# Row recurrence after a group norm: a second row of the first half inside the statistics stage, and a last row of the second half by itself

## The chip, the cores and the metric

The kernel runs on one core of a Trainium2 chip. A core has five engines with instruction queues of their own: TensorE (PE, matrix products; its weight loads are listed as PEld), VectorE (DVE), ScalarE (ACT), GpSimd (POOL) and SyncE (SP, which here only issues DMAs). Each engine works through its own instructions in the order in which they were written, and waits where an operand is not there yet. The metric is the time of one execution in device microseconds.

## The reference, cut to what matters

```python
x = x + conv_ref(gn(x), W_is, b_is, W_ss, b_ss)      # x: 8 x 96 x 128 x 128, float32

def gn(v):                     # group norm over (3 channels, all rows, all pixels) of one image, 32 groups
    return (v - mean) / sqrt(var + 1e-5)

def conv_ref(X, ...):
    its = masked 1x3 convolution of every row of X (96 -> 384 channels)
    h = c = 0
    for each of the 128 rows:  # a scan from top to bottom
        gates = conv1x3(h, W_ss) + its[row]           # 96 -> 384 channels along the row
        f, i, o = sigmoid(...); g = tanh(...)         # 96 channels each
        c = f * c + i * g
        h = o * tanh(c)
        out[row] = h
```

Two things set the shape of the work. The statistics of an image need all its pixels before the first row can be normalised. And the rows are a chain: the products of row r+1 need the h of row r, in all pixels and channels.

## The kernel before, in words

**Halves and half steps.** The eight images are two halves (s = 0: images 0 to 3, s = 1: images 4 to 7), which are independent chains. A row of one half is a half step; its index n counts both halves alternately, `n = 2 * row + s`, so n runs from 0 to 255. While one half waits for its activations, TensorE works on the other. One half step has a gate tile of 128 x 512 in each of three PSUM banks, A, B and C (forget, input and output gates, with a third of g in each). The pixels of a row are kept as even and odd halves of 256 columns (4 images x 64).

**A half step** (class `HalfStep`) consists of: the products of the normalised input P, Q, E (`p_`, `q_`, `t_`, tile xs); the products of h, "1" and "2" (with the sum vs and the difference vf of even and odd h, made by `total` S and `difference` F) and "0" and "3" (with the shifted differences vd, `shifted` D, on POOL); a copy cp of the bank's first half, and lo/hi, a sum and a difference that turn the bank into even and odd pixels (`copy`, `even`, `odd`); then ta and si (tanh, sigmoid on ACT), fg, gt, ce, th, ou (f times c, i times g, the new c, its tanh, h) and re (x plus h). All products are written in line 475, in float32; each matmul call shows as two instructions in the profile.

**The order of the work** is written out by hand and as strings. `PERIOD` is the order for one half step of the main loop, `LAST` that for the last: a name such as `3C'` is part 3 of bank C of the half step before, `''` two before, `+` the one after, `<` and `>` take the lower or upper 64 rows of TensorE, a and b are even and odd pixels. `W1`, `W2`, `W3`, `U` and `X` stand where the normalised rows of the next block of four rows are prepared (function `prepare`, lists `FIRST`, `LATER`, `SHARED`): on POOL (`widen`, `add_pixels`, `subtract_pixels`) and partly on ACT (line 308).

**The statistics stage.** Before the main loop every image is read once from HBM: six chunks of 1 MB for each (24 slots of 512 columns), in a ring of six buffers (line 938). A chunk's slots go through `bn_stats` on DVE (line 950), or a whole chunk through ACT (`sums_of`, lines 228 to 230, shares set by `by_act`: chunks 1 and 3 of each image). Of chunks 0, 2 and 4 TensorE picks the first rows (`pick_rows`, line 198). `aggregate` (line 854) ends an image. When the first four images are known, `Scale` makes their scale and shift (lines 264 to 302), and the first half step, n = 0, is run among the statistics of images 4 to 6; the products of n = 2 follow (`next_products`), so that n = 1 and n = 2 can start when the last image is known. Where these things stand is written in the table `events`: `at(i, m)` is the place after slot m of image i. `spin` and `keep_warm` (line 183) are products whose result nobody reads. After the loop `final.deviations()` is TensorE's first step for the last image.

**The main loop** is `do(n, PERIOD)` for n from 2 to 254, then `do(255, LAST)` and six calls behind it for the end of n = 255. In `LAST`, the end of n = 254 and all of n = 255 are interleaved.

Of the kernel before, what the change touches and what calls it, by code (L numbers as in the profile page):

```python
# [21 lines left out]
def kernel(  # L22
# [29 lines left out]
    nc = tc.nc  # L52
    B, C, H, W = x.shape
# [386 lines left out]
    class HalfStep:  # L440


        def __init__(self, n):
            self.n, (self.row, self.s) = n, divmod(n, NH)
# [113 lines left out]
        def sigmoid(self, a, lo=0, hi=BH, t=None):  # L558
            if self.row == 0 and a == 0:
                return  # L560
            gate = self.part(self.ps[a][0:C], lo, hi, t)
            if t == 0 and self.n > NH:
# [4 lines left out]
            nc.scalar.activation(to, gate, AF.Sigmoid)  # L567

        def forget(self):
            f = self.ps[0][0:C]  # L570
            if self.row > 0:
                nc.vector.tensor_mul(f, f, self.c)

        def gated(self, lo=0, hi=BH, t=None):
            to = self.g if self.row > 0 else self.c
# [53 lines left out]
            )  # L629
            hold(diff, self.last)  # L630

        def residual(self):
            s, row = self.s, self.row
            xo = xt[s, row // R][0:C, :, row % R, :].rearrange("p b (j t) -> p t b j", t=2)
            if self.n < NH or self.n == last - 1:
                nc.gpsimd.tensor_add(xo, xo, self.h)
            else:
                residuals.append(nc.vector.tensor_add(xo, xo, self.h))  # L638
# [28 lines left out]
    def beside(s, k, *images):  # L667
# [15 lines left out]
    def work(n):  # L683
        if n < len(FIRST):
            return FIRST[n]
        row, s = divmod(n, NH)
# [33 lines left out]

    def finish(n):
        prepare(n)
        row, s = divmod(n, NH)
# [24 lines left out]
    SPLIT = ("taC", "siB", "gt", "ce", "th", "ou")  # L748
    PARTS = {
# [12 lines left out]
    def do(n, names, by_lanes=False):  # L762

        for name in names.split():
            if name in "UX":
                if n >= NH:
                    prepare(n - NH, name)
# [19 lines left out]

            if part in ("S", "F", "D"):
                at += NH
            if not 0 <= at <= last:  # L790
                continue
            step = half_step(at)
            if name in step.done or whole_name in step.done:
# [9 lines left out]
            if by_lanes and part == "re":  # L803
                finish(at)


# [36 lines left out]
        step.shifted()  # L843
        step.done |= {"S", "F", "D"}

    def begin():
        operands(0)
        do(0, "PA PB QA QB PC QC 1A 2A 1B 2B 1C 2C")

    def at(image, n):  # L850
        return image * NS + n
# [29 lines left out]
        late[0].means()  # L881

    def keep_warm(count):
        unread = late[0].banks[0] if early_done else half_step(1).ps[1]
        spin(1, bst[:, done - 1, :], unread)
        spin(count, wt[0][:, 0:256], unread)
# [1 line left out]

    early_done = []
    events = {  # L890
        at(4, 5): lambda: (late.insert(0, Scale(0, 0, BH)), begin_scale()),
        at(4, 6): squares,
        at(4, 8): lambda: (
            late[0].scale(), late[0].shift(), [own_image(0, 0, j) for j in range(BH)]
        ),
        at(4, 13): lambda: shared_rows(nc.scalar, 0, 0, R),
        at(5, 4): begin,
        at(5, 6): lambda: do(0, "cpA cpB cpC"),
        at(5, 17): lambda: do(
            0, "loA hiA EA 0A 3A loB hiB EB 0B 3B loC hiC EC 0C 3C taA taB siB taC siC"  # L900
        ),
        at(6, 4): lambda: (do(0, "gt th ou"), operands(2), do(0, "re")),
        at(6, 6): next_products,
        at(6, 17): lambda: keep_warm(8),
        at(6, 22): lambda: do(2, "cpA cpB cpC"),
        at(7, 5): begin_scale,
        at(7, 7): squares,
        at(7, 8): lambda: (next_row(), spin(8, wt[0][:, 0:256], half_step(1).ps[1])),
        at(7, 12): next_operands,
        at(7, 16): lambda: spin(3, wt[0][:, 0:256], half_step(1).ps[1]),  # L910
        at(7, 20): lambda: (own_row(xw[1], 1, 0, 0, BH - 1), early("1A 2A 1B 2B"), keep_warm(1)),
        at(7, 21): lambda: keep_warm(1),
        at(7, 22): lambda: keep_warm(3),
        at(7, 23): lambda: keep_warm(1),
        at(7, 24): lambda: keep_warm(1),
    }
    for b in range(B - 1):
        events[at(b + 1, 7 if b == 4 else 5 if b == 5 else 4)] = lambda b=b: aggregate(b)
    stats = []
    n = m = 0  # L920
    load_weights()
# [3 lines left out]
    for b in range(B):  # L925
        bst = g_pool.tile([P, NS, 6], F32, tag="bst", name=f"bst{b}")
        records = bst.rearrange("c n s -> c (n s)")
        shares = by_act(b)
        own_stats = NS - sum(shares.values())
        stats.append(records[:, 0 : 6 * own_stats + 3 * len(shares)])  # L930
        xb = x[b].rearrange("c h w -> (c h w)").rearrange("(p q) -> p q", p=P)
        done = 0
        for k in range(QW // CH):
            xc = ring[n % len(ring)]
            pieces = 2 if n == B * QW // CH - 1 else 1
            for piece in range(pieces):
                size = CH // pieces
                nc.sync.dma_start(  # L938
                    xc[:, bass.ts(piece, size)], xb[:, bass.ds(k * CH + piece * size, size)]
                )  # L940
            n += 1
            if k % 2 == 0:
                pick_rows(b, k // 2, xc)
            alone = shares.get(k, 0)
            if alone:
                i = list(shares).index(k)
                sums_of(b, i, xc[:, CH - alone * SN :], records[:, 6 * own_stats + 3 * i :][:, 0:3])
            for j in range(CH // SN):
                if j < CH // SN - alone:
                    nc.vector.bn_stats(bst[:, done, :], xc[:, bass.ts(j, SN)])  # L950
# [68 lines left out]
    step.residual()  # L1019
    finish(last)  # L1020


# [52 lines left out]
```

## Time and profile before

| what | us |
|---|---|
| median of 3 runs (range) | 1966.6 (1965.81 to 1968.24) |
| the profiled execution, its own time | 1967.33 |
| its span in the profile | 1965.5 |
| last chunk of statistics begun by DVE | 128.87 |
| aggregate of the last image ends | 130.87 |
| TensorE's first product for the last image | 132.48 |
| last residual add ends | 1962.13 |

The profile lists busy times by engine, a chain of work that ended last, groups of instructions, and a timeline. A timeline row has the start in us, the duration, the engine, the line, the operation with its output and input tiles, shapes, how many instructions the row merges, and in brackets the idle time of the engine before it and what ended it. In a table by stretches each row has the stretch, its length, the busy time (and instructions) of PE, PEld, DVE, ACT and POOL, the granted clock of TensorE, the busy share of the DMA engines and GB/s.

### The profile page before, as it was taken

How to read it: one execution, taken by the hardware profiler on the slowest of the kernel's cores; microseconds unless marked ns; L12 is line 12 of the kernel's file. 1: busy time of each engine (PE TensorE's matmuls, PEld its weight loads, DVE VectorE, ACT ScalarE, POOL GpSimd, SP SyncE). 2: the span in 40 equal slices, each digit the busy share in tenths (PEclk: the TensorE clock that was granted, in tenths of full speed). 3: DMA queues.
4: the chain of work that ended last, by engine and by line, in shares of the span. 5: the costliest groups of instructions: out<-in, count | busy, mean ns of one | idle time of the engine just before them, and what ended most of it. 6: DMA issues, size and time to landing. Idle time of an engine off the chain costs nothing.

```text
span 1965.5 us, 46244 instructions
## 1 busy us (share of the span) xinstructions
PE 1901.2 (97%) x17492; PEld 1819.2 (93%) x17492; DVE 1794.7 (91%) x4002; ACT 1567.1 (80%) x3494; POOL 1359.4 (69%) x1645
## 2 busy tenths in 40 slices
PE   3699999999999999999999999999999999999998
PEld 0279999999999999999999999999999999999997
DVE  5778999999999999999999999999999999999998
ACT  6777888887888888888888877888887888888777
POOL 3348777777777777777777777777777777777752
PEclk9999999999999999999999999999999999999999
DMA  9993343444334334433433443343344433434411
GB/s 402 421 308 75 88 116 94 105 119 117 82 87 115 97 98 119 119 90 85 107 98 98 119 119 98 82 103 100 95 119 119 101 86 95 109 94 112 119 34 33
DMA packets 101277, 234.64 MB, mean 119 GB/s; under 512 B 5824, under 2 KB 7360, under 8 KB 95040
## 3 DMA queue, kind: packets, MB, share of 16 engines
q1 hardware_dynamic: 101056, 231.70, 43.6%
q8 instruction: 138, 2.26, 0.5%
q14 instruction: 83, 0.68, 0.1%
HBM read 181.34 MB, written 50.33 MB: 118 GB/s over the span
## 4 chain that ended last, share of the span: by engine, by line
PE 93%; DMA 4%; DVE 2%; ACT 1%; issue 0%; SPq 0%; POOL 0%; DVEq 0%; POOLq 0%; ACTq 0%
PE ps L475 92%; DMA xs<-in_x_dram 4%; DVE bst L950 1%; PE ps L183 0%; PE dm L183 0%; ACT g L555 0%; ACT piece L308 0%; DVE ps L551 0%; DVE hx L604 0%; DVE ps L547 0%; SPq L938 0%; DVE vf L621 0%; PE rows L198 0%; ACT th L596 0%; ACT ps L567 0%
## 5 line engine op out<-in xcount | busy, mean ns | idle before, releaser
L475 PE MATMUL ps<-vd,wl 64*128 64x256 f32 (+1 forms) x6092 | 1191.6, 376 | 0.1
L475 PEld LDWEIGHTS ps<-vd,wl 64*128 64x128 f32 (+1 forms) x6092 | 871.9, 186 | 16.7 <-issue 1.3
L475 PE MATMUL ps<-vs,wm 64*128 64x256 f32 (+1 forms) x3054 | 821.3, 376 | 2.4 <-POOL vs L617 2.3
L475 PE MATMUL ps<-vf,wm 64*128 64x256 f32 (+1 forms) x3056 | 766.8, 377 | 1.1 <-DVE vf L621 1.1
L475 PE MATMUL ps<-xs,wx 64*128 64x256 f32 (+1 forms) x3586 | 747.1, 347 | 0.4 <-POOL xs L327 0.4
L475 PEld LDWEIGHTS ps<-xs,wx 64*128 64x128 f32 x3586 | 606.5, 187 | 4.3 <-POOL xs L327 2.3
L567 ACT ACTIVATE ps<-ps 96x256 f32<-96x256 f32 (+1 forms) x767 | 387.8, 506 | 231.5 <-PE ps L475 223.0
L475 PEld LDWEIGHTS ps<-vs,wm 64*128 64x128 f32 (+1 forms) x3054 | 528.8, 186 | 12.9 <-POOL vs L617 2.7
L555 ACT ACTIVATE g<-ps 32x256 f32<-32x256 f32 (+1 forms) x1021 | 468.6, 482 | 25.0 <-PE ps L475 6.0
L475 PEld LDWEIGHTS ps<-vf,wm 64*128 64x128 f32 (+1 forms) x3056 | 459.4, 186 | 20.9 <-DVE vf L621 1.9
L475 PE MATMUL ps<-xs,wt 64*128 64x256 f32 x1528 | 452.8, 377 | 0.4 <-DVE ps L551 0.4
L543 ACT ACTIVATE m<-ps,wl 128x256 f32<-128x256 f32 x766 | 363.0, 474 | 95.0 <-PE ps L475 70.1
L625 POOL TENSOR_TENSOR vd<-hx 128x512 f32<-128x512 f32 x257 | 287.9, 1120 | 180.0 <-DVE vs L617 170.3
L547 DVE TENSOR_TENSOR ps<-m,ps 128x256 f32<-128x256 f32 x768 | 324.3, 423 | 78.8 <-ACT m L543 78.6
L551 DVE TENSOR_TENSOR ps<-m,ps 128x256 f32<-128x256 f32 x768 | 326.9, 426 | 18.7 <-PE ps L475 1.2
L638 DVE TENSOR_TENSOR x<-x,hx 96x512 f32<-96x512 f32 x253 | 341.0, 1348 | 0.0
L310 POOL TENSOR_SCALAR xw<-xr,rstd,nmr 128x512 f32<-128x512 f32 (+1 forms) x255 | 205.6, 806 | 115.0 <-DVE x L638 114.5
L310 POOL TENSOR_SCALAR hx<-x,rstd,nmr 32x512 f32<-32x512 f32 (+1 forms) x249 | 222.4, 893 | 72.9 <-POOL xs L331 52.7
L331 POOL TENSOR_TENSOR xs<-xw 128x512 f32<-128x512 f32 (+1 forms) x254 | 270.9, 1067 | 0.0
L475 PEld LDWEIGHTS ps<-xs,wt 64*128 64x128 f32 x1528 | 266.5, 187 | 2.0 <-DVE ps L551 1.6
L579 POOL TENSOR_TENSOR g<-i,g 96x256 f32<-96x256 f32 x252 | 183.5, 728 | 118.0 <-ACT g L555 110.1
L604 DVE TENSOR_TENSOR hx<-ps,th 96x256 f32<-96x256 f32 (+1 forms) x510 | 190.5, 413 | 1.9 <-ACT th L596 1.8
(101 smaller groups left out, 1505.5 us busy)
## 6 DMA issues: line engine op xcount, KB each, us to landing
xr<-in_x_dram SPq DMA_DIRECT2D x124, 512.0 KB, 6.5
x<-in_x_dram SPq DMA_DIRECT2D x62, 768.0 KB, 5.9
out_dram<-x SPq DMA_DIRECT2D x62, 768.0 KB, 5.2
xs<-in_x_dram SPq DMA_DIRECT2D x31, 1024.0 KB, 12.4
piece<-in_x_dram SPq DMA_DIRECT2D x16, 1024.0 KB, 10.8
x<-in_x_dram SPq DMA_DIRECT2D x62, 256.0 KB, 3.2
out_dram<-x SPq DMA_DIRECT2D x2, 576.0 KB, 3.7
xs<-in_x_dram SPq DMA_DIRECT2D x2, 512.0 KB, 13.3
```

The source lines that it names most:

```text
L310: return engine.tensor_scalar(dst, src, scale, shift, ALU.mult, ALU.add)
L331: nc.gpsimd.tensor_sub(differences, strided(xw[:, 0, :], 0, [(W + 1, n), (J, 2), (1, J)]), strided(xw[:, 0, :], J + 1, [(W + 1, n), (0, 2) ...
L475: made = nc.tensor.matmul(self.ps[a][:, bass.ts(half, HB)][:, cols], weights[rows, bass.ts(a, P)], rhs[rows, cols], start=new, stop=False, ...
L543: nc.scalar.activation(self.m1[a], m1, AF.Identity, bias=column)
L547: nc.vector.tensor_add(self.ps[a][:, 0:HB], self.m1[a], self.ps[a][:, HB:])
L551: nc.vector.tensor_sub(hi, self.m1[a], hi)
L555: nc.scalar.activation(self.part(g, lo, hi, t), self.part(ps, lo, hi, t), AF.Tanh)
L567: nc.scalar.activation(to, gate, AF.Sigmoid)
L579: nc.gpsimd.tensor_mul(to, i, g)
L604: nc.vector.tensor_mul(h, o, th)
L625: diff = nc.gpsimd.tensor_sub(self.operand("vd", 2)[:, :, lo:hi], strided(h, 1, [(BH * JP - 1, 2), (JP, hi - lo), (1, J)]), strided(h, 0, ...
L638: residuals.append(nc.vector.tensor_add(xo, xo, self.h))
```

## The change

1. The first half runs one row ahead of the second (`LEAD = 1`, function `place`): n = -2 and n = 0 are rows 0 and 1 of s = 0 and both stand among the statistics; n = 2 is row 2 of s = 0, beside n = 1, row 0 of s = 1. So n = 254 no longer exists, and the loop ends with n = 253; n = 255, row 127 of s = 1, has no partner.
2. Rows 0 to 3 of the first half are no longer prepared image by image (`own_image`, four rows each) but row by row (`row_of`).
3. The table of events is written anew. `next_products` moves from `at(6, 6)` to `at(7, 6)`. `keep_warm(1)`, four TensorE instructions, stands after every slot from `at(6, 12)` to `at(7, 22)`, but does nothing before `next_products`; the other spins of the loop are gone.
4. ACT takes other chunks: in image 4 and 7 chunks 0 and 3, in image 5 chunk 0 alone, in image 6 chunk 1 and half of chunk 3. The slots left over go to DVE.
5. `LAST` is a new order for the end of n = 253 and all of n = 255, with its steps split by even and odd pixels; its input products (P, Q, E) stand ahead of h, and E is added to both halves of the bank with half weights. The six calls behind the loop are gone.

```diff
     def by_act(b):
-        return {1: CH // SN, 3: CH // SN}
+        shares = (
+            {1: 4, 3: 4},
...
+            {0: 4, 3: 4},
+            {0: 4},
+            {1: 4, 3: 2},
+            {0: 4, 3: 4},
+        )
+        return shares[b]
...
+    LEAD = 1
+
+    def place(n):
+
+        row, s = divmod(n, NH)
+        return row + (LEAD if s == 0 else 0), s
...
         def t_(self, a):
-            if self.n >= last - 1:
-                self.mm(a, 0, wh, self.xs[:, 2].rearrange("p b j -> p (b j)"))
-            else:
+            if 0 < self.n < last:
                 self.own(a, 2)
+                return
+            rhs = self.xs[:, 2].rearrange("p b j -> p (b j)")
+            rows = slice(C2, P) if a == order["B"] else slice(0, C2)
+            for half in range(2):
+                self.mm(a, half, wh, rhs, rows)
...
-        ([], own(1, 1, 3), [(load_rows, 1, 2)]),
+        (shared(0, 2, *SHARED[0]), own(1, 1, 3), [(load_rows, 1, 2)]),
         ([], own(0, 2, 0), []),
     ]
-    LATER = dict(zip((9, 11, 13), own(1, 2, 0, 1)))
+    LATER = dict(zip(range(8, 14), own(0, 2, 1, 1) + own(1, 2, 0, 1)))
...
     LAST = (
-        "1A hiC' D'' siBb' 1B siBa' 2A siA' 2B re'' 0C' taA' taB' 3C' EC' fg' cpA loA cpB 2C loB 1C "
-        "taCa' hiA taCb' hiB gta' siC' gtb' 0A 3A EA cpC ceb' 0B 3B EB cea' loC hiC 0C 3C EC "
-        "taA siA thb' tha' siB taB fg oub' oua' re' taC siC gt"
+        "0C'' 3C'' EC'' siBa'' taA'' re''' taB'' taCa'' gta'' PB taCb'' siBb'' QC QB fg'' PA "
+        "gtb'' cea'' QA PC siC'' tha'' ceb'' oua'' thb'' oub'' EA EB EC F'' S'' D'' re'' 1A "
+        "2A 1B 1C 2B 2C cpA loA hiA cpB loB 3A hiB 0A 0B 3B cpC loC hiC 0C 3C taA siA fg taB "
+        "siBa siBb taCa taCb gta gtb siC ceb cea thb tha oub oua rea reb"
     )
...
+    def row_of(s, r):
+        for j in range(BH):
+            widen(nc.gpsimd, xw[r % 2], j, 1, s, 0, j, r)
+        own_row(xw[r % 2], s, r)
...
     def keep_warm(count):
+        if not early_done and 1 not in steps:
+            return
...
-        at(6, 4): lambda: (do(0, "gt th ou"), operands(2), do(0, "re")),
-        at(6, 6): next_products,
-        at(6, 17): lambda: keep_warm(8),
-        at(6, 22): lambda: do(2, "cpA cpB cpC"),
-        at(7, 5): begin_scale,
-        at(7, 7): squares,
-        at(7, 8): lambda: (next_row(), spin(8, wt[0][:, 0:256], half_step(1).ps[1])),
-        at(7, 12): next_operands,
-        at(7, 16): lambda: spin(3, wt[0][:, 0:256], half_step(1).ps[1]),
-        at(7, 20): lambda: (own_row(xw[1], 1, 0, 0, BH - 1), early("1A 2A 1B 2B"), keep_warm(1)),
...
+        at(5, 17): lambda: (do(-2, "siB"), do(-2, "taC"), do(-2, "gt"), do(-2, "siC")),
+        at(5, 18): lambda: (do(-2, "th"), do(-2, "ou"), operands(0)),
...
+        at(6, 20): lambda: (do(0, "taC"), do(0, "gt"), do(0, "siC"), do(0, "ce"), do(0, "th")),
+        at(6, 22): lambda: (do(0, "ou"), operands(2), do(0, "re")),
+        at(7, 6): lambda: (aggregate(6), next_products(), begin_scale()),
+        at(7, 8): lambda: (squares()),
+        at(7, 9): lambda: (do(2, "cpA")),
+        at(7, 12): lambda: (do(2, "cpB"), next_row()),
+        at(7, 17): lambda: (do(2, "cpC")),
+        at(7, 19): lambda: (next_operands(), own_row(xw[1], 1, 0, 0, BH - 1)),
+        at(7, 22): lambda: (early("1A 2A 1B 2B")),
     }
...
+                if at(6, 12) <= m <= at(7, 22):
+                    keep_warm(1)
...
-    for n in range(2, last):
+    for n in range(2, last - 1):
         do(n, PERIOD, by_lanes=True)
     do(last, LAST, by_lanes=True)
-    step, halves = half_step(last), [(0, BH // 2), (BH // 2, BH)]
-    for at in halves:
-        step.cell(*at)
-        step.cell_tanh(*at)
-    for at in halves:
-        step.output(*at)
-    step.residual()
     finish(last)
```

(The new events are written here on one line each; the places and calls are those of the kernel.)

More of the change, by code (lines that the diff above doesn't have):

```diff
@@ L747 @@
     IMAGES = {"l": (0, BH // 2), "h": (BH // 2, BH)}
-    SPLIT = ("taC", "siB", "gt", "ce", "th", "ou")
+    SPLIT = ("taA", "taB", "taC", "siA", "siB", "siC", "fg", "gt", "ce", "th", "ou", "re")
     PARTS = {
@@ L789, in do @@
                 at += NH
-            if not 0 <= at <= last:
+            if place(at)[0] >= NT:
                 continue
@@ L890 @@
     events = {
[L891 to L892 removed]
+        at(2, 0): lambda: (
+            aggregate(0),
+        ),
+        at(2, 13): lambda: (
+            aggregate(1),
+        ),
+        at(3, 8): lambda: (
+            aggregate(2),
+        ),
+        at(4, 3): lambda: (
+            aggregate(3),
+            late.insert(0, Scale(0, 0, BH)), begin_scale(),
+        ),
+        at(4, 4): lambda: (
+            squares(),
+        ),
@@ L893 @@
+        at(4, 5): lambda: (
+            late[0].scale(), late[0].shift(),
+        ),
+        at(4, 7): lambda: (
+            row_of(0, 0),
+        ),
         at(4, 8): lambda: (
-            late[0].scale(), late[0].shift(), [own_image(0, 0, j) for j in range(BH)]
-        ),
[L896 to L900, printed above, removed]
-        ),
@@ L912 @@
[L912 to L915, printed above, removed]
-    }
-    for b in range(B - 1):
-        events[at(b + 1, 7 if b == 4 else 5 if b == 5 else 4)] = lambda b=b: aggregate(b)
+            shared_rows(nc.scalar, 0, 0, R),
+            operands(-2),
+        ),
+        at(4, 10): lambda: (
+            do(-2, "PA PB QA QB PC QC EA EB EC"),
+        ),
+        at(4, 15): lambda: (
+            do(-2, "1A 2A 1B 2B 1C 2C"),
+            do(-2, "cpA"),
+            do(-2, "cpB"),
+        ),
@@ new lines @@
+        at(4, 16): lambda: (
+            do(-2, "cpC"),
+        ),
+        at(4, 18): lambda: (
+            row_of(0, 1),
+            row_of(0, 2),
+            row_of(0, 3),
+        ),
+        at(5, 3): lambda: (
+            do(-2, "loA hiA"),
+            do(-2, "0A 3A"),
+            do(-2, "loB hiB"),
+        ),
+        at(5, 4): lambda: (
+            do(-2, "0B 3B"),
+            do(-2, "loC hiC"),
+        ),
+        at(5, 8): lambda: (
+            do(-2, "0C 3C"),
+        ),
@@ new lines @@
+        at(5, 9): lambda: (
+            do(-2, "taA"),
+        ),
+        at(5, 14): lambda: (
+            do(-2, "taB"),
+        ),
+        at(5, 15): lambda: (
+            aggregate(4),
+        ),
+        at(5, 17): lambda: (
+            do(-2, "siB"),
+            do(-2, "taC"),
+            do(-2, "gt"),
+            do(-2, "siC"),
+        ),
+        at(5, 18): lambda: (
+            do(-2, "th"),
+            do(-2, "ou"),
+            operands(0),
+        ),
+        at(5, 21): lambda: (
+            do(-2, "re"),
+        ),
@@ new lines @@
+        at(5, 22): lambda: (
+            do(0, "PA PB QA QB PC QC EA EB EC"),
+            do(0, "1A 2A 1B 2B 1C 2C"),
+        ),
+        at(6, 3): lambda: (
+            do(0, "cpA"),
+        ),
+        at(6, 4): lambda: (
+            do(0, "cpB"),
+        ),
+        at(6, 5): lambda: (
+            do(0, "cpC"),
+            do(0, "loA hiA"),
+            do(0, "0A 3A"),
+        ),
+        at(6, 7): lambda: (
+            do(0, "loB hiB"),
+            do(0, "0B 3B"),
+        ),
+        at(6, 8): lambda: (
+            aggregate(5),
+        ),
@@ new lines @@
+        at(6, 12): lambda: (
+            do(0, "loC hiC"),
+        ),
+        at(6, 14): lambda: (
+            do(0, "0C 3C"),
+            do(0, "taA"),
+        ),
+        at(6, 16): lambda: (
+            do(0, "siA"),
+        ),
+        at(6, 19): lambda: (
+            do(0, "fg"),
+            do(0, "taB"),
+            do(0, "siB"),
+        ),
+        at(6, 20): lambda: (
+            do(0, "taC"),
+            do(0, "gt"),
+            do(0, "siC"),
+            do(0, "ce"),
+            do(0, "th"),
+        ),
@@ new lines @@
+        at(6, 22): lambda: (
+            do(0, "ou"),
+            operands(2),
+            do(0, "re"),
+        ),
+        at(7, 6): lambda: (
+            aggregate(6),
+            next_products(),
+            begin_scale(),
+        ),
+        at(7, 8): lambda: (
+            squares(),
+        ),
+        at(7, 9): lambda: (
+            do(2, "cpA"),
+        ),
+        at(7, 12): lambda: (
+            do(2, "cpB"),
+            next_row(),
+        ),
+        at(7, 17): lambda: (
+            do(2, "cpC"),
+        ),
```

47 lines of the change are left out of this document (30 added, 17 removed).

## The prediction, made before the changed kernel ran

> **What bounds the kernel now.** I read the page first, then the table by stretches, then the timeline around the two ends. The page names the bound of nearly the whole span: TensorE is busy for 97% of it, and the chain that ended last is 93% PE and 4% input DMA.
>
> ```profile
> span 1965.5 us, 46244 instructions
> PE 1901.2 (97%) x17492; PEld 1819.2 (93%) x17492; DVE 1794.7 (91%) x4002; ACT 1567.1 (80%) x3494; POOL 1359.4 (69%) x1645
> PE 93%; DMA 4%; DVE 2%; ACT 1%; issue 0%; SPq 0%; POOL 0%; DVEq 0%; POOLq 0%; ACTq 0%
> ```
>
> In the main loop PE has no gap (50.00 of 50 us), and DVE is near its limit too (46.77). Two outputs h that follow each other stand 7.20 us apart (1925.85, 1933.05): that is a half step, 68 PE instructions. During the statistics the DMA engines are full (share 1.01) and everything else has room: of the 14.9 to 15.4 us that six chunks need, DVE is busy for 10.5 to 13.6 and PE for 11.0 to 13.2.
>
> ```profile
> 300.00:350.00 50.00, 50.00 (x480) 48.95 (x480) 46.77 (x106) 40.51 (x93) 36.74 (x43) 1.00 0.41 105
> 1925.85 0.74 DVE L604 TENSOR_TENSOR hx<-ps,th 96x256 f32<-96x256 f32 x2
> 1933.05 0.75 DVE L604 TENSOR_TENSOR hx<-ps,th 96x256 f32<-96x256 f32 x2
> 78.52:93.45 14.93, 11.04 (x30) 5.68 (x30) 10.51 (x17) 13.60 (x18) 11.20 (x21) 1.00 1.01 421
> 93.45:108.81 15.36, 12.62 (x54) 8.25 (x55) 13.62 (x25) 13.40 (x20) 4.21 (x7) 1.00 1.01 419
> 108.81:123.77 14.96, 13.24 (x55) 10.16 (x54) 12.12 (x28) 14.01 (x19) 5.02 (x19) 0.89 1.01 418
> ```
>
> The end of the statistics is where the profile surprises. DVE is on time: it waits for the first chunk of the last image (0.20 us) and for the last one (1.44), and its aggregate ends at 130.87. But PE takes up the last image only at 132.48. It was not waiting for DVE; it was working off its own queue of unread products, which is a part of the chain from 118.97 on.
>
> ```profile
> 113.96 2.47 DVE L950 BATCH_NORM_STATS2 bst<-xs 128x6 f32<-128x512 f32 x4 [0.20 <-DMA xs<-in_x_dram]
> 118.97 5.22 PE ps L183 x16
> 128.34 0.28 PE L183 MATMUL dm<-bst,wl 128*128 128x6 f32 x2
> 128.87 1.29 DVE L950 BATCH_NORM_STATS2 bst<-xs 128x6 f32<-128x512 f32 x2 [1.44 <-DMA xs<-in_x_dram]
> 129.00 0.28 PE L183 MATMUL dm<-bst,wl 128*128 128x6 f32 x2
> 130.26 0.61 DVE L854 BATCH_NORM_AGGREGATE st<-bst 128x2 f32<-128x102 f32 x1
> 132.48 0.28 PE L264 MATMUL dm<-st,wl 128*128 128x1 f32 x2
> ```
>
> So three places decide: the steady half step, the moment at which PE begins the last image (132.48), and the tail.
>
> **What the change removes.** Half step 254 goes: the loop runs one PERIOD less, and n = 253 is at the same number of half steps behind the statistics as before. All gain is therefore in the tail, and the statistics can only hide the moved half step or lose time on it.
>
> **The tail.** Before, h of n = 253 is complete at 1948.18 and the last residual ends at 1962.13: 13.95 us, in which n = 254 is interleaved with 255.
>
> ```profile
> 1947.44 0.74 DVE L604 TENSOR_TENSOR hx<-ps,th 96x256 f32<-96x256 f32 x2
> 1948.22 0.42 DVE L621 TENSOR_TENSOR vf<-hx 128x256 f32<-128x256 f32 x1
> 1948.56 0.42 DVE L617 TENSOR_TENSOR vs<-hx 128x256 f32<-128x256 f32 x1
> 1949.23 1.51 DVE L638 TENSOR_TENSOR x<-x,hx 96x512 f32<-96x512 f32 x1
> 1951.77 1.13 PE L475 MATMUL ps<-vd,wl 128*128 128x256 f32 x4
> 1951.87 0.48 DVE L541 TENSOR_SCALAR m<-ps,wl 128x256 f32<-128x256 f32 x1 [0.53 <-PE ps L475]
> 1952.39 0.76 DVE L547 TENSOR_TENSOR ps<-m,ps 128x256 f32<-128x256 f32 x2
> 1953.37 0.65 ACT L555 ACTIVATE g<-ps 32x256 f32<-32x256 f32 x2 [0.98 <-PE ps L475]
> 1955.26 0.59 ACT L555 ACTIVATE g<-ps 32x512 f32<-32x512 f32 x1
> 1955.88 0.57 ACT L567 ACTIVATE ps<-ps 96x512 f32<-96x512 f32 x1
> 1961.44 0.69 DVE L638 TENSOR_TENSOR x<-x,hx 96x512 f32<-96x512 f32 x1
> ```
>
> Now the same chain alone, from h of 253 on, in the order of the new LAST: S and F 0.80 (1948.18 to 1948.98); `re''`, which stands ahead of cpA on DVE, 1.51 (2.3 so far); cpA 0.48, loA and hiA 0.76 (3.55); 3A and 0A 1.1 (4.65); on PE banks B and C follow by 0.9 each (5.5, 6.4). ACT then is what ends last: taA 0.59, siA 0.57, taB 0.59 (6.4), siB in two halves, 0.37 each by my estimate from 0.57 for twice the pixels (7.15), taC in halves 0.65 (7.8). Behind it go the halves of gt, ce, th, ou and re; by 0.35 to 0.4 us each, half of the 0.69 to 0.75 of the whole rows above, seven steps of one half and its neighbour come to 2.6. Sum 10.4, so 3.6 less than 13.95. The input products P, Q, E are ahead of h and cost nothing here: they run on PE while ACT and DVE finish n = 253. Their cover is that chain (over 3 us against 26 instructions of about 0.2). Further, h of 253 itself comes earlier. The PERIOD of 253 loses the 16 PE instructions that belonged to 254 (16 x 7.20 / 68 = 1.7 us), and then nothing of 254 stands between. From 0 (DVE, at 94%, hardly lets it shorten) to 2; I take 1.0. Tail: -4.6, between -3.5 and -6.
>
> **The statistics: prices.** What stands behind the forecast is the queue of PE in the last image. Its prices in this trace:
>
> ```profile
> 83.52 2.08 PE L198 MATMUL rows<-xs,pick 128*128 128x512 f32 x2 [2.91 <-DMA xs<-in_x_dram]
> 114.36 1.02 PE L198 MATMUL rows<-xs,pick 128*128 128x512 f32 x2
> 100.82 0.95 PE L264 MATMUL pv<-eps,wl 128*128 128x3 f32 x8
> 101.70 1.99 PE L475 MATMUL ps<-xs,wx 64*128 64x256 f32 x12
> 106.01 0.70 PE L475 MATMUL ps<-vs,wm 128*128 128x256 f32 x2 [2.32 <-POOL vs L617]
> 108.53 0.59 PE L475 MATMUL ps<-vf,wm 128*128 128x256 f32 x2
> 117.09 0.36 PE L264 MATMUL dm<-st,wl 128*128 128x3 f32 x2 [1.72 <-DVE st L854]
> 127.04 0.49 PE L475 MATMUL ps<-vs,wm 128*128 128x192 f32 x2
> 110.82 3.70 PE L183 MATMUL ps<-wl 128*128 128x256 f32 x16
> ```
>
> `next_products` moves from image 6 into slot 6 of image 7. It stands behind the pick of chunk 0 of that image, which lands at 113.96 as before. From there PE must do, in order: the pick 1.02; the eps products 0.95; P and Q of n = 2, 1.99; "1" and "2" of n = 2, 2.7 (106.01 to 108.7); deviations, squares and means 1.9 (117.09 to the spins at 118.97); seventeen `keep_warm(1)`, from slot 6 to 22, each 0.66 (128.34 to 129.00), 11.2; the picks of chunks 2 and 4, 2.0; `early` 1.3 (127.04 to 128.34). That is 23.1 (the pick included), so `final.deviations()` comes at 137.0 even if PE never waits: 4.5 later than 132.48. The spins removed (16 at 118.97, 24 instructions from 128.34 on) are in 132.48 already. As long as this queue lasts, DVE may end its slots up to 6 us later than its 130.87 at no cost of its own.
>
> **The statistics: waits.** DVE gets more work in images 5 and 6, from these rows and 0.69 for gt, fg, ce and ou of the whole width:
>
> ```profile
> 108.81 4.96 DVE L950 BATCH_NORM_STATS2 bst<-xs 128x6 f32<-128x512 f32 x8 [0.73 <-DMA xs<-in_x_dram]
> 105.31 0.64 POOL L617 TENSOR_TENSOR vs<-hx 128x256 f32<-128x256 f32 x1 [8.72 <-DVE hx L604]
> 105.91 0.74 POOL L621 TENSOR_TENSOR vf<-hx 128x256 f32<-128x256 f32 x1
> ```
>
> A slot is 0.62. Image 5: 20 slots 12.4, aggregate 0.6, six lo/hi 2.4, gt and ou 1.4: 16.8. Image 6: 18 slots 11.2, 0.6, 2.4, fg, gt, ce, ou 2.8: 17.0. The chunks of an image come in 14.95, so DVE, which was on time at 113.96, is 3.9 late there; and gt waits in order for ACT's tanh, ou for th, which I put at 2.4 (from 0 to 4; in the trace such an ou waited 0.9). Then it ends image 6 at 120.3, ou of n = 0 (two slots before) at 119.0, and S and F on POOL give vf at 120.4. The "1" and "2" products and all that is behind them on PE, 2.7 + 1.9 + 11.2 + 2.0 + 1.3 = 19.1, end at 139.5. PE also starts that work at half speed: the same 16 spins took 3.70 at 110.82 and 5.22 at 118.97, where the clock was granted at 0.50:
>
> ```profile
> 120.00:121.00 1.00, 1.00 (x4) 0.82 (x3) 0.90 (x4) 0.97 (x3) 0.18 (x1) 0.50 1.00 418
> ```
>
> That is 1.5 more: 141.0, 8.5 later than before. The Trainium skill, "TensorE: Matmul & The Clock Gate", Part 1, says that an idle window of about 3.4 us puts the array to half clock, and a busy one of that length releases it. By the page the extra would be an estimated 1.7 in place of 1.5, and the whole sum 0.2 higher; the 0.50 in the row agrees, how PE's gaps lie in the new order no run here shows yet.
>
> ACT and POOL. ACT gets the seven activations of the extra row, about 4 us, and three copies, and gives up six of its chunk units; its busiest image, the fourth, comes to some 15 us and delays only buffers (below). `row_of` for four rows costs POOL 14 us where `own_image` cost 10; it has 11.2 busy of 14.93 at most, and the rows are wanted one by one. SP keeps its order; the prefetch of x waits for chunk 0 of image 7, now read by ACT, some 3 us later, and is not read before about 145. Behind the statistics n = 1 and n = 2 run the same steps, shifted. In the loop the first new block of s = 0 comes two half steps sooner; the ACT part (`X`) of its last image then stands directly ahead of F': once 0.3 us, from 0 to 0.9.
>
> **Sum.** Against the profiled execution, 1967.33 (0.7 above the median of 1966.6): +8.5 +0.3 -4.6 = +4.2, that is 1971.5, or 1970.8 for the median. The half step of 7.2 is saved in number, 2.6 of it is lost because the last row is alone, and 8.5 go to the queue ahead of the last image.
>
> **The rivals.**
> - *No waits, only the queue.* If DVE keeps up (ou of n = 0 by 116), PE's own 23.1 decide: +4.5 +0.3 -4.6 = +0.2, 1966.8. For it: DVE's extra work is placed where ACT has the chunk. Against: 16.8 and 17.0 of 14.95.
> - *The move is hidden.* The last image begins at 132.5 as before, which needs that the seventeen pairs run in gaps that I do not see, or cost a third: +0.3 -4.6, 1962.3, faster. For it: the spins ahead of the aggregate in slots 23 and 24 are gone, and 1.6 us lay idle between 130.87 and 132.48. Against: the sum of PE's rows.
> - *The input DMA starves.* SP issues in ring order; a buffer that is given back more than five chunks (12.4 us) after its landing stops the reads. ACT's shared rows, chunk 3 of image 4 and three copies that wait for PE stand ahead of chunk 0 of image 5, which I put back at 10 us after landing. From 2.4 us more on, each is paid in full; with 5.4 more it is +3 on top of the forecast, 1973.8.
>
> **How the numbers follow.** About 0.2% (3.9 us) is what a measurement of this kernel can tell from no change. Forecast 0.33, starved DMA 0.12, no waits 0.33, hidden 0.22. Slower: 0.33 + 0.12 = 0.45; same 0.33; faster 0.22. The forecast lies just over the bound of 1970.5, so its own range, 1968 to 1973, reaches into "same". The range goes from 1961 (the hidden case with a tail 1.3 better) to 1976 (the starved case and 2 more); what is left out is some 0.15.
>
> **What the profile after would show.** The first product of the last image (L264 on st, one column) near 141.0; at 137 the waits are wrong, at 132.5 the queue. A row of L183 pairs without gaps ahead of it would show the queue. DVE's aggregate of the last image by then long ended. n = 253's h to the last residual in 10 to 11 us instead of 13.95. The share of DMA under 1 between 95 and 115 would show starving. The prediction is wrong if PE takes up n = 2's products much earlier than 119, or if the half step is no longer 7.20.

## The result, and the profile after

The changed kernel takes 1975.15 us (median of 6 runs, 1972.82 to 1978.11), the kernel before 1966.2 in the same comparison (1964.96 to 1968.24). The ratio is 1.0045, with a 95% interval of 1.0033 to 1.0058: slower by about 0.45%. Ratios here and below leave slow executions aside; there was one each of e3_xr_first and e4_both (5383.74 and 2530.08 us), which count in their medians alone. The profiled execution took 1974.58 us, with a span of 1972.8; its counterpart before took 1967.33, with a span of 1965.5. So the two traces differ by 7.3 us. I take them apart at three marks: TensorE's first product for the last image, the h of n = 1 and of n = 251, and the end of the span.

The timeline of the changed kernel at the end of the statistics (start, duration, engine, line, operation and tiles, instructions, in brackets the idle time before and what ended it; `dm` on `st` with one column is the first product of the last image):

```profile
115.43 1.10 PE L198 MATMUL rows<-xs,pick 128*128 128x512 f32 x2 [1.32 <-DMA xs<-in_x_dram]
118.64 0.67 DVE L623 TENSOR_TENSOR hx<-ps,th 96x512 f32<-96x512 f32 x1
120.09 0.70 PE L491 MATMUL ps<-vs,wm 128*128 128x256 f32 x2 [0.86 <-POOL vs L636]
...
127.43 0.28 PE L183 MATMUL ps<-bst,wl 128*128 128x6 f32 x2
128.08 0.28 PE L183 MATMUL ps<-bst,wl 128*128 128x6 f32 x2
...
132.68 0.62 DVE L880 BATCH_NORM_AGGREGATE st<-bst 128x2 f32<-128x102 f32 x1
136.80 0.49 PE L491 MATMUL ps<-vs,wm 128*128 128x192 f32 x2
138.76 0.28 PE L274 MATMUL dm<-st,wl 128*128 128x1 f32 x2
139.07 0.28 DVE L295 TENSOR_SCALAR q<-dm,st 128x1 f32<-128x1 f32 x1 [5.78 <-PE dm L274]
```

The reader is to see two delays here. DVE's last aggregate starts 2.4 us later than before (132.68 against 130.26). And PE, which used to take up the image 1.6 us after the aggregate's end, now does so 5.5 us after it (133.30 to 138.76). All that time it is working off its own queue without a gap: five pairs of L183, 0.65 us apart, the first products of n = 1 (`early`, 1.3 us) and one more pair. DVE waits 5.78 us.

The timeline of the changed kernel's tail, h (`hx`) and the last half residual:

```profile
153.57 0.69 DVE L623 TENSOR_TENSOR hx<-ps,th 96x512 f32<-96x512 f32 x1 [0.70 <-ACT th L615]
...
1944.83 0.74 DVE L623 TENSOR_TENSOR hx<-ps,th 96x256 f32<-96x256 f32 x2
1952.02 0.74 DVE L623 TENSOR_TENSOR hx<-ps,th 96x256 f32<-96x256 f32 x2
1957.61 0.75 DVE L623 TENSOR_TENSOR hx<-ps,th 96x256 f32<-96x256 f32 x2 [0.15 <-ACT th L615]
1968.64 0.76 DVE L655 TENSOR_TENSOR x<-x,hx 96x256 f32<-96x256 f32 x2
```

From the end of h of n = 253 (1958.36) to the end of the last residual (1969.40) it is 11.04 us; it was 13.95. The h of n = 1 before, for the account (that of n = 251 stood at 1933.05):

```profile
147.29 0.69 DVE L604 TENSOR_TENSOR hx<-ps,th 96x512 f32<-96x512 f32 x1 [0.70 <-ACT th L596]
```

| part | before | after | difference |
|---|---|---|---|
| first product of the last image | 132.48 | 138.76 | +6.3 |
| first product to h of n = 1 | 14.81 | 14.81 | 0 |
| h of n = 1 to h of n = 251, 250 half steps | 1785.76 | 1791.26 | +5.5 |
| h of n = 251 to the end of the span | 32.45 | 27.97 | -4.5 |

The third row is the surprise. In the changed kernel most half steps take 7.13 us, but between 300 and 1800 us ten of them take 7.3 to 8.04. The timeline of the changed kernel around the longest, about n = 120: two h 8.04 us apart; then SP's DMA issues, POOL's row that waits, and SP's wait for the store in the view of the waits (engine, line, waited for, us in total, times, longest):

```profile
992.86 0.74 DVE L623 TENSOR_TENSOR hx<-ps,th 96x256 f32<-96x256 f32 x2
1000.90 0.74 DVE L623 TENSOR_TENSOR hx<-ps,th 96x256 f32<-96x256 f32 x2
...
981.92 0.33 SPq L664 DMA_DIRECT2D out_dram<-x  x1
982.83 0.59 SPq L160 DMA_DIRECT2D xr<-in_x_dram  x1
987.14 0.32 SPq L168 DMA_DIRECT2D x<-in_x_dram  x1
...
987.98 0.60 SPq L160 DMA_DIRECT2D xr<-in_x_dram  x1
...
997.65 0.81 POOL L320 TENSOR_SCALAR xw<-xr,rstd,nmr 128x512 f32<-128x512 f32 x1 [2.04 <-DMA xr<-in_x_dram]
...
SPq L168 <- DMA out_dram<-x: 3.7, 1, 3.7
```

POOL, which widens the next rows, waits 2.04 us for a load of `xr`. The halves stand one row apart now. So the end of a block of s = 0 (store of `x`, load of the block after the next into the same buffer) and the load of `xr` for s = 1 fall into the same half step. The load of `x` has to wait for the store (3.7 us), and the second half of `xr` stands behind it on SP: 987.98, 5.2 us after the first half.

### The profile page after: what moved, and what is told of

Read it like the earlier page. It is cut to its first block, busy times and chain, and to the rows that moved or that the text cites. A ratio compares the mean times of both kernels' runs of the same rounds, so it can differ in the third digit from the quotient of the medians.

```text
span 1972.8 us, 46228 instructions
## 1 busy us (share of the span) xinstructions
PE 1907.3 (97%) x17480; PEld 1820.1 (92%) x17480; DVE 1794.4 (91%) x4006; ACT 1559.4 (79%) x3489; POOL 1358.6 (69%) x1654
## 5 line engine op out<-in xcount | busy, mean ns | idle before, releaser
L491 PE MATMUL ps<-xs,wx 64*128 64x128 f32 (+1 forms) x3582 | 746.0, 348 | 2.2 <-POOL xs L337 2.1
L586 ACT ACTIVATE ps<-ps 96x512 f32<-96x512 f32 (+1 forms) x768 | 388.1, 506 | 227.4 <-PE ps L491 219.0
L574 ACT ACTIVATE g<-ps 32x256 f32<-32x256 f32 (+1 forms) x1021 | 468.1, 481 | 22.5 <-PE ps L491 3.8
L615 ACT ACTIVATE th<-c 96x256 f32<-96x256 f32 (+1 forms) x509 | 191.1, 418 | 7.1 <-DVE c L610 6.5
```

The costliest lines, as they stand in the source:

```text
L491: made = nc.tensor.matmul(self.ps[a][:, bass.ts(half, HB)][:, cols], weights[rows, bass.ts(a, P)], rhs[rows, cols], start=new, stop=False, ...
L574: nc.scalar.activation(self.part(g, lo, hi, t), self.part(ps, lo, hi, t), AF.Tanh)
L615: nc.scalar.activation(self.part(self.th, lo, hi, t), self.part(self.c, lo, hi, t), AF.Tanh)
```

## The experiments

Each is compared with the kernel before, run on the same chip in the same call. "First product" is that of the last image, "loop" the time from h of n = 1 to h of n = 251.

| kernel | median us | ratio to before [95%] | last aggregate | first product | h of n = 1 | loop |
|---|---|---|---|---|---|---|
| changed kernel | 1975.15 | 1.0045 [1.0033, 1.0058] | 132.68 | 138.76 | 153.57 | 1791.26 |
| e1_no_spins | 1972.98 | 1.0031 [1.002, 1.0043] | 136.55 | 137.22 | 155.44 | 1791.13 |
| e2_late_spins | 1973.71 | 1.0037 [1.0025, 1.005] | 136.56 | 141.10 | 155.91 | 1791.42 |
| e3_xr_first | 1971.62 | 1.002 [1.001, 1.0029] | 136.13 | 142.20 | 157.02 | 1786.42 |
| e4_both | 1967.7 | 1.0008 [0.9999, 1.0017] | 134.81 | 136.01 | 150.83 | 1786.40 |
| e5_e_late | 1962.57 | 0.9984 [0.9975, 0.9993] | 131.06 | 132.26 | 147.09 | 1785.71 |
| e6_chunk1 | 1969.68 | 1.002 [1.001, 1.0029] | 136.40 | 139.28 | 154.08 | 1785.68 |
| e7_e_late_chunk1 | 1962.66 | 0.999 [0.9981, 0.9999] | 131.03 | 131.93 | 146.75 | 1785.76 |
| e8_even_spins | 1962.17 | 0.9982 [0.9973, 0.9991] | 131.00 | 132.09 | 146.90 | 1785.66 |
| e9_e_late_alone | 1972.01 | 1.003 [1.0018, 1.0042] | 131.51 | 137.58 | 152.38 | 1790.14 |
| e10_e_late_xr | 1967.2 | 1.0008 [0.9999, 1.0016] | 130.99 | 137.06 | 151.87 | 1785.61 |

**The pairs.** `e1_no_spins` takes all 17 `keep_warm` pairs away:

```diff
-                if at(6, 12) <= m <= at(7, 22):
-                    keep_warm(1)
```

> The changed kernel without its seventeen keep_warm pairs among the statistics; the rest is unchanged. If the queue of unread products delays the last image (theory), PE takes it up right behind DVE's aggregate, near 133.6 instead of 138.76, and the kernel gains 5; the PE steps behind it may start at half clock, which gives back up to 1.7. So 3.5 to 5 us faster than the changed kernel. If DVE's extra slots are what makes the last image late (rival), the aggregate at 133.3 is the bound and PE's queue only fills the gap: less than 1 us. If the input loads in the loop matter as well, their share of some 5 us stays in both cases.

`e2_late_spins` keeps those of the last six slots:

```diff
-                if at(6, 12) <= m <= at(7, 22):
+                if at(7, 17) <= m <= at(7, 22):
                     keep_warm(1)
```

> The changed kernel with keep_warm only behind slots 17 to 22 of the last image, six pairs instead of seventeen. Theory (queue): eleven pairs of 0.66 are 7.2 us less on PE, more than it is late (138.76 against DVE's 133.3), so the last image begins near 134 with a warm array: 4.5 to 5 us faster than the changed kernel, and not slower than without any pair. Rival (DVE): less than 1 us.

In e1 the wait behind the aggregate is gone: it ends at 137.17, and PE's first product starts at 137.22. Nearly nothing of it reaches the loop, though. From the first product to h of n = 1 it is 18.22 us instead of 14.81, since PE works at half clock. Table by stretches of e1 (stretch, length, busy time of PE, PEld, DVE, ACT and POOL with instructions, granted clock, DMA share, GB/s):

```profile
130.00:135.00 5.00, 1.02 (x4) 0.50 (x2) 4.66 (x15) 4.16 (x9) 3.09 (x10) 0.80 1.07 196
135.00:140.00 5.00, 5.00 (x19) 4.47 (x18) 2.72 (x8) 0.00 (x0) 2.12 (x4) 0.50 1.06 220
```

In e2 the pairs themselves ran at half rate, after an idle time in front of the first: four of the six in full, the first in part; timeline of e2:

```profile
132.46 0.36 PE L183 MATMUL ps<-bst,wl 128*128 128x6 f32 x2 [1.92 <-DVE bst L1104]
134.71 0.43 PE L183 MATMUL ps<-bst,wl 128*128 128x6 f32 x2
135.99 0.43 PE L183 MATMUL ps<-bst,wl 128*128 128x6 f32 x2
```

They follow each other at 1.28 us (134.71 to 135.99) instead of 0.65. So the pairs have a use, and neither run shows what the queue of 17 costs. Both show something else besides: the aggregate starts at 136.55, 3.9 us later than in the trace of the changed kernel. The same is seen in e3 below (136.13), whose front is not edited at all. So the front of the changed kernel differs from execution to execution; where, is seen under "The input". The trace above is of an execution of middling length (the third of six), those of e1 to e3 are of long ones.

**The late load in the loop.** `e3_xr_first` holds the store and the reload of s = 0 back until the `xr` load of s = 1 is issued (the 17 pairs stay); `e4_both` joins it to the late pairs of e2:

```diff
+            if part is load_rows:
+                release()
...
+    held = []
+
+    def release():
+        while held:
+            s, k = held.pop(0)
+            store(s, k, 0, R)
+            load(s, k + 2)
...
     def finish(n):
         prepare(n)
+        release()
         row, s = place(n)
         k, r = divmod(row, R)
-        if r == R - 1:
+        if r == R - 1 and s == 0 and 0 < k < NB - 2:
+            held.append((s, k))
+        elif r == R - 1:
```

> The changed kernel; only the DMA order in the loop is different: store and load of x of the first half, at the end of a block, are issued behind the xr load of the second half, which in the changed kernel comes in the same half step. Theory: the irregular half steps of the loop (up to 8.04 instead of 7.13, one in each block, 5.6 us in all) come from POOL waiting for that xr load, which SP issues behind an x load that itself waits for the store; so all half steps come to 7.13 to 7.20 and the kernel gains 5 to 5.5. The last image begins at 138.8 as before. Rival: the stall comes from POOL having too much work in that half step, then nothing changes (within 1 us).

> Six pairs only and the xr load first, both edits at once. Theory: the two losses are independent and add: 9.5 to 10.5 us faster than the changed kernel, so about 1.5 us faster than the kernel before. If either theory falls, only the other one's 5 us show and it stays slower than before.

SP's issues in e3, the same place:

```profile
983.71 0.34 SPq L664 DMA_DIRECT2D out_dram<-x  x1
984.63 2.32 SPq L160 DMA_DIRECT2D xr<-in_x_dram  x2
989.03 0.32 SPq L168 DMA_DIRECT2D x<-in_x_dram  x1
```

Both halves of `xr` go out together, POOL's waits for `xr` are gone from the view of the waits, and the loop falls to 1786.42, 4.8 us less; in e5 to e8 and e10, which have the same edit, it is 1785.6 to 1785.8, as before. That settles the third row of the account. e4, with few pairs besides, has a warm clock (its pairs are 0.65 apart) and starts the last image 1.2 us after the start of the aggregate; its time is that of the kernel before (interval 0.9999 to 1.0017). Its aggregate is still 4.5 us later than before, and this is the third loss.

**The input.** The DMA engines do starve, and that was taken for the cause. Tables by stretches of the changed kernel and of e4:

```profile
90.00:95.00 5.00, 4.03 (x15) 2.39 (x13) 5.00 (x10) 4.89 (x6) 4.26 (x10) 1.00 0.93 372
95.00:100.00 5.00, 3.93 (x25) 3.02 (x24) 3.89 (x7) 4.74 (x7) 0.27 (x1) 1.00 0.90 321
```

```profile
90.00:95.00 5.00, 5.00 (x19) 3.21 (x17) 4.58 (x9) 4.37 (x7) 3.72 (x8) 1.00 0.59 203
95.00:100.00 5.00, 4.44 (x25) 3.11 (x25) 4.76 (x9) 4.89 (x7) 0.71 (x3) 1.00 0.91 326
```

Before, about 420 GB/s were moved from 60 to 120 us. Two reasons were open: TensorE's late pick of image 4's chunk 4, which stands behind P, Q and E of row 0 (timeline of the changed kernel),

```profile
77.90 3.95 PE L491 MATMUL ps<-xs,wx 64*128 64x256 f32 x12 [1.74 <-POOL xs L337]
81.65 3.59 PE L491 MATMUL ps<-xs,wh 64*128 64x256 f32 x12
87.86 1.88 PE L198 MATMUL rows<-xs,pick 128*128 128x512 f32 x4
88.91 6.90 SPq L1091 DMA_DIRECT2D xs<-in_x_dram  x4
```

and ACT, which reads chunk 0 of image 5 late. `e5_e_late` is e4 with the E products of rows 0 and 1 of the first half behind the transform, as they were before; there they are half as many, too:

```diff
-            if 0 < self.n < last:
+            if self.n < last:
                 self.own(a, 2)
...
-            do(-2, "PA PB QA QB PC QC EA EB EC"),
+            do(-2, "PA PB QA QB PC QC"),
...
-            do(-2, "0A 3A"),
+            do(-2, "EA 0A 3A"),
```

> e4 with one more edit: for the rows among the statistics the E products stand behind the bank's transform, with 0 and 3, as in the kernel before (6 instructions for a row, not 12 ahead of it). Theory: the input reads starve between 90 and 100 us because the pick of chunk 4 of image 4 on PE (at 87.9 in the changed kernel) stands behind 12 own and 12 E products at half clock, and SP issues in ring order; without the E products (3.6 us) the pick comes at 84.3, the DMA keeps 400 GB/s or more from 85 to 100, and DVE's last aggregate comes at 131 to 132.5 where e4 had 134.8: 2 to 3.5 us faster than e4. Rival: the buffer that SP waits for is the one that ACT reads late (chunk 0 of image 5); then the gap in the reads stays at 95 and less than 1 us is gained.

`e6_chunk1` is e4 with ACT's share of image 5 moved from chunk 0 to chunk 1, and `e7_e_late_chunk1` has both:

```diff
-            {0: 4},
+            {1: 4},
```

> e4 with the share of image 5 moved: ACT takes chunk 1 where it took chunk 0. By the theory of the late pick nothing is gained (PE still picks chunk 4 of image 4 behind the cold products), within 1 us of e4. By the rival (ACT reads chunk 0 of image 5 late and holds its buffer) the reads no longer starve at 95 to 100 and 1 to 2.5 us are gained.

> Both edits on e4. If each holds a buffer back in turn, only both together keep the reads at full rate: DVE's last aggregate near 131, 3 to 4 us faster than e4, that is 1 to 2 us faster than the kernel before. If the pick alone counts, the same as e5.

The table by stretches of e5, and of e6:

```profile
90.00:95.00 5.00, 4.87 (x16) 2.35 (x15) 5.00 (x10) 4.90 (x7) 4.25 (x11) 1.00 1.00 395
```

```profile
90.00:95.00 5.00, 5.00 (x19) 3.23 (x17) 4.97 (x10) 4.34 (x7) 3.76 (x8) 1.00 0.59 210
95.00:100.00 5.00, 4.34 (x25) 2.98 (x25) 2.55 (x5) 4.89 (x7) 0.71 (x3) 1.00 1.02 431
```

With E late the input keeps its pace, the last aggregate starts at 131.06, and the span is 1960.8 instead of e4's 1965.2. The kernel is now faster than the one before: 0.9984 [0.9975, 0.9993]. The ratio falls by 0.0024 against e4, which is 4.7 us. Moving ACT's share alone gains nothing. In e6 the reads recover from 95 us on (431 GB/s against e4's 326), as that rival said, and yet the aggregates of images 5 and 6 start at 110.39 and 123.76, where e4 has 110.37 and 123.74.

So E is the cause, but the input is not the way. The view of the waits has all that DVE waited for between 84 and 131 us, in e4, then in e5; the last row is its wait for the input in the kernel before:

```profile
DVE ps L566 <- ACT m L562: 4.8, 3, 3.6
DVE c L600 <- ACT g L574: 1.1, 1, 1.1
```

```profile
DVE ps L566 <- ACT m L562: 1.3, 3, 0.8
DVE c L600 <- ACT g L574: 1.1, 1, 1.1
```

```profile
DVE bst L950 <- DMA xs<-in_x_dram: 5.9, 5, 2.5
```

In neither does DVE wait for a load. It waits for ACT: for the copies of row 0's banks, which wait for the products "1" and "2" on TensorE behind E, and for a tanh. ACT's queue holds, in this order, these copies, a copy of the rows that TensorE picks right behind "1" and "2", a chunk of the statistics, and that tanh. DVE's step behind the tanh starts 10.9 us after the pick in both (100.86 and 97.13), and from there to the last aggregate DVE has no idle time in which to catch up. So the last aggregate follows from the start of the pick of image 4's chunk 4, if DVE's wait for TensorE's means behind image 6 is added where there is one (us):

| trace | pick | DVE's wait for TensorE | last aggregate | aggregate less both |
|---|---|---|---|---|
| changed kernel | 87.86 | 0 | 132.68 | 44.82 |
| e3_xr_first | 89.33 | 1.94 | 136.13 | 44.86 |
| e4_both | 89.98 | 0 | 134.81 | 44.83 |
| e5_e_late | 86.24 | 0 | 131.06 | 44.82 |
| e6_chunk1 | 90.00 | 1.54 | 136.40 | 44.86 |
| e9_e_late_alone | 86.68 | 0 | 131.51 | 44.83 |

Both columns also hold what differs between executions, and it is TensorE's rate. In the changed kernel's trace the 12 instructions of E take 3.59 us in row 0 and 1.89 in row 1, so TensorE begins row 0 at half rate. There it is at full rate from the first of "1" and "2" on (0.59 to 0.70 us for a pair of instructions), in e4's trace only from the last (1.06 to 1.22 before it). The clock column stands at 1.00 there in both; it is the durations that show the rate. And in e3's trace the clock is 0.50 when the means behind image 6 are due:

```profile
120.00:125.00 5.00, 5.00 (x14) 3.54 (x12) 4.87 (x9) 4.90 (x7) 4.04 (x7) 0.50 1.01 423
```

**Where the pairs stand.** `e8_even_spins` is e7 with eight pairs, one after every second slot from 8 to 22 of the last image:

```diff
-                if at(7, 17) <= m <= at(7, 22):
+                if at(7, 8) <= m <= at(7, 22) and m % 2 == 0:
                     keep_warm(1)
```

> e7 with eight keep_warm pairs, behind every second slot from 8 to 22 of the last image, in place of six behind 17 to 22. Theory: what PE needs ahead of the last image is no gap over some 3 us, not a full queue; in e2 PE stood still before slot 17 and its pairs then took 1.28 us instead of 0.66. With the pairs spread, the granted clock stays 1.0 from 120 to 140 in every execution and the time is the same as e7's best, with less spread. Rival: eight pairs queue up behind next_products again and the last image begins 1 to 2 us later than in e7.

1962.17 us; no difference from e5 can be told. With the aggregate on time, six or eight pairs do equally well in these two places.

**One edit at a time.** The price of the 17 pairs was still mixed with the late aggregate. `e9_e_late_alone` is the changed kernel with the E edit of e5 and nothing else; `e10_e_late_xr` has the order of loads of e3 besides. So e10 differs from e5 in the pairs alone.

> The changed kernel, with one edit: the E products of rows -2 and 0 stand behind the transform again, so that the pick of image 4's chunk 4 comes about 2 us sooner on TensorE. All 17 pairs and the order of the loop's loads stay. Theory (late pick starves the input, the queue of pairs is a separate 4 to 5 us, the late loads in the loop a third one of 4.9): the input stays near 420 GB/s from 85 to 100 us, the last aggregate starts near 131, but the last image's first product still waits for the pairs, near 137, so first h near 151.8; loop 1791.3; profile near 1970.4 and median near 1971. Rival (the starved input was all of the front's loss, and with chunks on time the pairs run in gaps): first product near 132.5, first h near 147.1, time near 1967.

> The same, and in the loop the load of xr goes out ahead of the other half's store. All 17 pairs stay: against e5 it differs only in the number of pairs (17 against 6). Theory: first product near 137, first h near 151.8, loop 1786.4; median 4 to 5 us over e5, near 1967. Rival (pairs run in gaps): as e5, 1962.6.

Timeline of e10, then of e5:

```profile
113.93 1.10 PE L198 MATMUL rows<-xs,pick 128*128 128x512 f32 x2 [0.67 <-DMA xs<-in_x_dram]
130.99 0.62 DVE L893 BATCH_NORM_AGGREGATE st<-bst 128x2 f32<-128x102 f32 x1
137.06 0.28 PE L274 MATMUL dm<-st,wl 128*128 128x1 f32 x2
```

```profile
126.96 0.36 PE L183 MATMUL ps<-bst,wl 128*128 128x6 f32 x2 [1.78 <-DVE bst L1117]
131.06 0.62 DVE L893 BATCH_NORM_AGGREGATE st<-bst 128x2 f32<-128x102 f32 x1
132.26 0.28 PE L274 MATMUL dm<-st,wl 128*128 128x1 f32 x2
```

The aggregates are at one place, the first products 4.8 us apart, and the medians 4.6 us (1967.2 against 1962.57). Eleven pairs at 0.65 are 7.2 us of PE; 1.8 of these lay idle in e5. That the pairs run in gaps is refuted. e9, with the loop as changed, is at 1972.01, 4.8 us over e10. The steps from the changed kernel to e5 are then, in ratios, with 1966 us for 1: E early 0.0015 or 2.9 us (1.0045 to 1.003), the order of loads 0.0022 or 4.3 (4.8 by the medians of this one call), eleven pairs 0.0024 or 4.7. Each of these differences is about as wide as its interval; the executions of the four kernels do not overlap, though (1972.82 and more, 1970.38 to 1972.31, 1966.62 to 1967.84, 1961.81 to 1963.09). In the traces of the changed kernel and of e9 the first step is 1.2 us at the h of n = 1, where the queue of pairs hides part of a late aggregate.

## Why the prediction was right or wrong

Slower was forecast, and it is slower; 1975.15 lies inside the range of 1961 to 1976, 4.4 us over the forecast of 1970.8 and outside the 1968 to 1973 of the forecast by itself. By steps, against the profiled execution (+4.2 forecast, +7.3 found):

- **The tail: right.** Forecast -4.6, found -4.5. Two small misses cancel in it: the chain alone takes 11.04 (forecast 10.4), and h of 253 is 1.6 us nearer to that of 252 (5.59 apart instead of the 7.20 of the last half steps before; forecast 1.0). Over the whole loop before, a half step was 7.14 (1785.76 by 250), not 7.20. In e5, where front and loop are those of before, this is what is left: h of n = 251 at 1932.80 and a span of 1960.8 make 28.0 against 32.45.
- **PE's queue: right.** The 23.1 us from the pick of the first chunk to the first product are 23.13 in e10 (113.93 to 137.06) and 23.33 in the changed kernel (115.43 to 138.76); 0.66 and 0.86 of these are a wait for POOL, so the queue without waits is 22.5. The floor of 137.0 is what e10 shows. It was the rival "No waits, only the queue" that had this case, and e10 is 1967.2 by its median, where that rival put 1966.8.
- **The front as a whole: +6.3 instead of +8.5 in this trace, and its waits were right.** DVE is late as forecast: h of n = 0 ends at 119.31 (forecast 119.0), TensorE's first product behind it waits for POOL and starts at 120.09 (forecast 120.4), and what follows takes 18.67 us (forecast 19.1). Not all of DVE's waits are those named: only 1.1 us are for ACT's tanh, and 2.7 are for the copies of row 0. The term that did not come is "PE also starts that work at half speed", 1.5 us. It depends on the execution: in the changed kernel's trace the clock is full, in e3's, whose front is not edited, it is 0.50, the same work takes 20.46 us (121.74 to 142.20), and the front costs +9.7.
- **The loop: wrong, and the step that failed is "once 0.3 us", with "SP keeps its order" and no word on SP's queue in the loop.** Found +5.5. I looked at what is done for the extra row and not at what the offset of one row brings together: a load that waits for a store, and the other half's load of `xr` behind it in the same queue. e3 shows it, by 4.8 us. The 0.3 itself is not seen: with the loads in the other order the loop of e5 is 1785.71, before 1785.76.
- **"The input DMA starves": its sign came, its mechanism did not.** The reads fall under 420 GB/s as that rival said, but in the traces of the changed kernel, e4 and e5 DVE waits for none of them up to the last aggregate, and ACT's late chunk 0 of image 5, which I had blamed, is excluded by e6. What costs is E on TensorE, ahead of what ACT, and behind it DVE, wait for. I costed its early place in the first rows at nothing, since I spoke of E only for the last row. The rival's price was +3 on top of the forecast; E early costs 2.9 with the 17 pairs behind it and 4.7 with six.
- **"The move is hidden": right as to what the change could bring.** 1962.3 was forecast for it. e5 and e8 give 1962.57 and 1962.17, once E, the order of loads and the number of pairs are mended.

That the time is inside the range is partly luck: 2.2 us too much at the front stand against 5.2 too little in the loop.

## What to carry to other kernels

When two chains are shifted against each other, list per step what each issues on every in-order queue, DMA queues too: a load that waits for its buffer holds up what stands behind it. Count filler work on an in-order engine as real work up to the next thing that matters, and put no more of it there than fits between a known idle time and that thing. Put work that has time behind what another engine waits for and not ahead of it: where that engine has no idle time left, each us that it waits comes out at the end. And before a starved input is called the cause, look whether the engine that is late ever waits for a load.

## What the runs showed of the hardware

The granted clock fell after less idle time than I had thought, and not always. In e2 and e4 PE was idle for the same 1.92 us ahead of the first pair; timeline of e4, then the clock by stretches of e2 and of e1:

```profile
130.70 0.36 PE L183 MATMUL ps<-bst,wl 128*128 128x6 f32 x2 [1.92 <-DVE bst L1117]
131.43 0.28 PE L183 MATMUL ps<-bst,wl 128*128 128x6 f32 x2
```

```profile
132.00:133.00 1.00, 0.54 (x3) 0.52 (x4) 1.00 (x3) 0.93 (x3) 1.00 (x3) 0.96 1.08 209
...
139.00:140.00 1.00, 1.00 (x6) 1.00 (x5) 0.00 (x0) 0.00 (x0) 0.00 (x0) 0.62 0.97 209
```

```profile
132.00:133.00 1.00, 0.00 (x0) 0.00 (x0) 1.00 (x3) 0.93 (x3) 1.00 (x3) 0.99 1.11 221
...
146.00:147.00 1.00, 1.00 (x4) 0.55 (x3) 0.00 (x0) 0.00 (x0) 0.90 (x2) 0.68 0.49 88
```

In e4 the pairs run at full rate, in e2 at half. The rows give the moments of the changes, as estimates: a stretch of 1 us at 0.96 was at full clock for 0.92 of it and at 0.50 for the rest. So e2 falls at 132.92 and comes back at 139.76, 6.84 us later, with PE busy all that time. e1 falls at 132.98 and comes back at 146.64, 13.66 us later, though PE was at work again from 134.50 on. In the kernel before, the half clock of which the prediction shows one row lasts 3.4 us (118.8 to 122.2). These are two steps of 3.4 us, four, and one. The Trainium skill, "TensorE: Matmul & The Clock Gate", Part 1, asks for at least one idle window of about 3.4 us for the fall and at least one busy window for the way back, and says that the window runs free, so that runs differ. The steps and the spread between e2 and e4 agree with it; a fall after 1.92 us without work does not agree with a whole idle window, and here the measurement decides. Where in a step the idle time lies may be what parts e2 from e4; no run tests it.
